# A literal order of pieces re-arranged in nine places, and idle products put in front of six waits of TensorE

## The chip, the cores and the metric

The kernel runs on one core of a Trainium2 chip. A core has TensorE (PE in the profile; its weight loads are PEld), VectorE (DVE), ScalarE (ACT), GpSimd (POOL) and SyncE (SP), and 16 DMA engines that all DMA queues share. The metric is device time in microseconds (us); lower is better. The kernel before was run four times: 711.54, 711.60, 713.12 and 713.61 us, median 712.36 us.

## The reference

Two feed-forward layers stand one behind the other, each behind a small conditioning step chosen by a number per batch. There are 8 batches of 512 tokens with 256 features.

```python
x = x + ffn0(cond0(x, lang0))     # low-rank products + embedding; int8-like rounding by one max over ALL of x and ALL of h
x = x + ffn1(cond1(x, lang1))     # adapter + layer norm; 9 experts, each token goes to its best 2
def ffn1(x):
    topk_w, topk_idx = top_k(softmax(x @ Wr), 2);  topk_w /= topk_w.sum()
    gate = silu(einsum('th,ehi->tei', xf, Wg));  hidden = gate * einsum('th,ehi->tei', xf, Wu)
    return einsum('tei,eih,te->th', hidden, Wd, cw)
```

Two facts set the shape of the work. The first layer's rounding of `h` needs one maximum over all batches, so nothing behind it can begin before the whole first half is done. And the second layer needs only 2 of 9 experts a token, so the kernel sorts tokens into lists by expert in DRAM and works on blocks of 128 list rows.

## The kernel before

**The front** (list `FRONT`, 8 batches in 4 pairs) makes the low-rank step, finds the maximum, rounds, and computes gate and up products (`gp`, `up`) into four PSUM tiles `wide` used in turn. `sl` and `uc` (ACT), `st` (DVE, L519) and `pm` (POOL) make `h`, and `mx` (DVE, L316) its maxima. At its end DVE joins the maxima (`htop_own`, L539), PE transposes that column (`across`, L320), a stretch of `ZEROS_BEHIND` idle products follows (`z`, L335: products of a tile of zeros into the `wide` tile that is next in turn), and DVE makes `htop` (L544) and the scale that every rounding of `h` needs.

**The literal order** (list `ORDER`) is a string of names written out by hand; each name runs one small function, and each engine gets its instructions in the order of the string. No planner changes it; semaphores follow from what each instruction reads and writes. The names, with batch b or block i behind them:

- `qa` (ACT, L624) and `qd` (DVE, L628) round `h`; `dp` (PE, L640) is the down product, `dv` (DVE, L647) adds it to x.
- `ap aa xp xa zp` make the adapter and the tokens' transposes (`xp` L693, `zp` L718), `zv` (DVE, L732) the norm's statistics, `np` (POOL, L739) and `nv` (DVE, L746) its scale, `na` (ACT, L756) and `nw` (DVE, L768) the normed rows, `tp` (PE, L776) and `ta` (ACT) their transposes.
- `cp ce ct cv` make the logits and the best two experts (`cv`, DVE, writes `both`, L830); `hp` (PE, L848 to L855) counts places from `both` and from `sofar`, `hv` (DVE, L861 to L874) makes the slots and the new `sofar`; `ca` writes the rows' tags.
- `hg` (POOL, L880) scatters 128 rows twice, by an indirect DMA each, into the DRAM tensor `lists`. There are 32 names, 64 DMAs.
- `pp`, `pw` plan which expert each block of 128 rows belongs to (`pp0b` is L959).
- For a block i: `R` (SP, L1052 to L1060) loads the block's place from SBUF into a register and issues five DMAs from `lists`; `U` and `W` (SP, L1067 and L1077) issue the expert's weights, 1408 KB and 768 KB, skipped when they are in place; `t` (DVE, L1088) transposes the rows; `g` in parts a, b, c (PE, L1098) is gate and up; `va vb vc vd` make `hidden`; `d` (PE, L1146) is the down product, `y` (DVE, L1152) weighs it, and `s` (POOL, L1156) adds the 128 rows to the output by an indirect DMA.

Blocks 0 to 13 are in the string; the others follow in a plain loop with the same pieces. Resources that bind names to each other:

```python
banks_sb = [psum.tile([P, 512], F32, name=f"bank{k}") for k in range(6)]   # dp ap tp cp ct hp pp g d, in turn
y_sb = [where_h_was(1, D) for _ in range(3)]                                # block i uses y_sb[i % 3]
...
nc.vector.tensor_scalar(y_sb[i % 3], held.pop(("po", i))[:, :D], ...)       # y, L1152
nc.gpsimd.indirect_dma_start(out=out, ..., in_=y_sb[i % 3], compute_op=ALU.add)   # s, L1156
own, `hg`:  out=own_rows[...]          # 64 disjoint views of `lists`
`R`:        lists[ds(r, P), quarter]   # a place known only at run time: any row of `lists`
```

So `y5` may write only when the transfer of `s2` has read the same tile, `y6` only behind `s3`. An `R` must wait for every `hg` that stands ahead of it in the string to have landed, and an `hg` for every `R` ahead of it to have read. One `s` waits for the landing of the one before it, since both add to `out`. SP has eight DMAs in the air at most, POOL also eight.

Of the kernel before, what the change touches and what calls it, by code (L numbers as in the profile page):

```python
# [32 lines left out]
P = 128  # L33
# [17 lines left out]
    up_2_3 mx_2_1 sl_2_3 up_2_4 mx_1_3 uc_2_3 up_3_0 st_2_4 gp_2_5 uc_3_0 pm_2_3 gp_3_0 mx_2_4 sl_2_5 up_2_5 up_3_1  # L51
    sl_3_0 st_2_5 gp_3_2 mx_2_5 uc_3_1 pm_3_0 mx_2_2 gp_3_1 sl_3_2 up_3_2 mx_2_3 sl_3_1 up_3_4 st_3_2 gp_3_5 pm_3_1
    uc_3_4 up_3_3 mx_3_0 sl_3_5 gp_3_4 mx_3_2 gp_3_3 sl_3_4 mx_3_1 up_3_5 sl_3_3 pm_3_4 st_3_5 st_3_3 mx_3_3 mx_3_4
    mx_3_5
"""
LAST_LOAD = "L_dT"
ZEROS_BEHIND = 12
ORDER = """
    qa0d fa1 fa0 fa2 qa0b qd0d qa0a qd0b qa0c fg0 fg1 qd0a qa2b qd0c dp0b qa1b qa1a dp0a qd1b dv0b qd1a dv0a dp1b
    qd2b qa2a xp0_1 dv1b xp0_0 ap0 xa0_1 qd2a xa0_0 dp1a qa2c xs0 aa0 qd2c qa4a zp0_0 dv1a zp0_1 zv0_0 qa3b ap1 fa3  # L60
    zv0_1 qa3a dp2a qd3b np0 aa1 qd3a dp2b dv2a pu1 pd0 nv0 dp3a dv2b na0_1 qd4a pu2 na0_0 nw0_1 xp1_1 ap2 qa4c
    xa1_1 nw0_0 xp1_0 qa4b zp1_1 dv3a xa1_0 tp0_0 pu0 aa2 zv1_1 zp1_0 ta0_0 qd4b tp0_1 qa5b zv1_0 dp3b ta0_1 qd4c
    np1 qa6b cp0 dv3b xs1 dp4b qd5b ce0 qa5a nv1 fa4 ct0 ap3 dv4b na1_1 mz0 cv0 dp4a na1_0 qa6c pd2 xp2_0 aa3 pd1
    xp2_1 nw1_1 hp0 ca0 fg2 xa2_1 hv0 tp1_1 xa2_0 zp2_1 ta1_1 xs2 nw1_0 hg0_0 zp2_0 zv2_1 tp1_0 fa5 ta1_0 zv2_0
    hg0_2 cp1 qd5a ce1 dv4a ct1 fg3 cv1 dp5b hg0_1 ap4 qd6b ca1 hp1 dv5b np2 aa4 dp5a hv1 qa6a hg0_3 nv2 pp0a qa7a
    pw0a dv5a pp0b pw0b na2_1 ap5 hg1_1 qd6a na2_0 pp0c qd6c nw2_1 dp6b qa7b hg1_3 nw2_0 xp3_1 xp3_0 xa3_1 pw0c fg4
    tp2_0 xa3_0 zp3_1 ta2_0 hg1_2 dv6b xs3 tp2_1 zv3_1 zp3_0 ta2_1 U0 qd7b cp2 aa5 zv3_0 hg1_0 ce2 fa6 dp6a qd7a
    ct2 dp7a dv6a np3 cv2 U1 dp7b W1 ap6 nv3 ca2 R0 dv7b na3_1 hp2 dv7a na3_0 xp4_0 hv2 xa4_0 xp4_1 nw3_0 R1 zp4_0
    xa4_1 zp4_1 nw3_1 tp3_0 aa6 t0 tp3_1 ta3_0 zv4_1 g0a W0 ta3_1 xs4 w0 zv4_0 fa7 cp3 va0 t1 hg2_1 g0b ce3 w1 fg5
    ct3 g0c vb0 np4 cv3 U2 g1a vc0 hg2_0 W2 nv4 g1b ca3 U3 vd0 va1 na4_1 hg2_2 g1c vb1 na4_0 nw4_1 d0 vc1 U4 hg2_3  # L70
    nw4_0 vd1 tp4_1 y0 xp5_0 ta4_1 s0 xp5_1 xa5_0 tp4_0 xa5_1 fg6 zp5_0 ta4_0 zp5_1 zv5_0 W3 cp4 zv5_1 ap7 ce4 R2
    ct4 np5 hp3 aa7 cv4 xs5 hv3 ca4 R3 nv5 hp4 hv4 na5_0 na5_1 t2 xp6_1 R4 w2 g2a xa6_1 nw5_0 nw5_1 tp5_0 va2 zp6_1
    ta5_0 t3 R5 d1 w3 zv6_1 t4 w4 tp5_1 y1 R6 xp6_0 ta5_1 s1 g2b xa6_0 zp6_0 vb2 W4 cp5 zv6_0 R7 g2c ce5 np6 g3a t5
    vc2 w5 nv6 vd2 ct5 xs6 na6_0 g3b U5 cv5 na6_1 d2 va3 fg7 hg3_3 nw6_1 ca5 nw6_0 hp5 W5 hg3_1 tp6_1 g3c hv5 ta6_1
    y2 tp6_0 vc3 U6 t6 xp7_0 hg4_0 ta6_0 w6 xp7_1 vb3 xa7_0 xa7_1 vd3 zp7_0 pp1a hg5_3 zv7_0 cp6 g4a ce6 pw1a xs7
    hg4_1 pp1b va4 g4b pw1b pp1c vb4 hg3_0 g4c pw1c d3 t7 vc4 U7 w7 hg3_2 vd4 g5a y3 W6 s2 d4 va5 hg4_3 g5b y4 W7
    s3 g5c vb5 hg4_2 g6a vc5 U8 vd5 hg5_2 g6b va6 g6c vb6 hg5_0 d5 vc6 U9 vd6 hg5_1 zp7_1 y5 ct6 W8 g7a zv7_1 s4
    cv6 d6 np7 va7 R8 nv7 ca6 na7_0 g7b s5 y6 na7_1 nw7_0 R9 hp6 g7c hv6 tp7_0 nw7_1 vc7 s6 ta7_0 R10 t8 tp7_1 w8
    g8a vb7 ta7_1 vd7 t9 d7 va8 w9 U10 R11 g8b y7 t10 s7 w10 cp7 vb8 g8c ce7 R12 ct7 g9a vc8 cv7 g9b va9 W10 t11
    ca7 U11 vd8 g9c w11 vb9 hg6_2 W9 d8 t12 vc9 w12 vd9 U12 hg6_1 g10a y8 W11 g10b s8 va10 hg6_3 g10c vb10 d9 vc10  # L80
    U13 vd10 hg6_0 g11a y9 W12 s9 d10 va11 R13 g11b y10 s10 g11c vb11 R14 g12a vc11 vd11 t13 d11 va12 w13 U14 R15
    g12b t14 y11 s11 g12c vb12 W14 hp7 vc12 R16 g13a hv7 vd12 pp2a va13 g13b pw2a R17 pp2b vb13 d12 pw2b W13 pp2c
    y12 U15 g13c pw2c s12 W15 vc13 hg7_3 U16 vd13 hg7_0 hg7_1 hg7_2
"""
BLOCKS_IN_ORDER = 14

# [2 lines left out]
def adaln_ffn_kernel(  # L89
# [21 lines left out]
    nc = tc.nc  # L111

    B, _, KC, S = xT.shape
# [21 lines left out]
    def act_scale(top, sig, name):  # L135
# [27 lines left out]
    start = rt.tile([P, NJ, E], F32, name="start")  # L163
    nc.gpsimd.iota(
        start, pattern=[[0, NJ], [CAP, E]], base=0, channel_multiplier=0, allow_small_or_imprecise_dtypes=True
# [13 lines left out]
    wdT = l0.tile([P, NM, D], BF16, name="wdT")  # L179
# [26 lines left out]
    turn_of = {}  # L206
# [35 lines left out]
    with tc.tile_pool(name="hw", bufs=1) as hw, tc.tile_pool(  # L242
# [75 lines left out]
        def across(pi, col, n, i):  # L318

            nc.tensor.transpose(pi[:, i : i + n], col.to_broadcast([n, P]), ident[:n, :n])  # L320
# [9 lines left out]
        @front  # L330
        def z(n):

            pz = wide_sb[(turn_of.get("wide", -1) + 1) % len(wide_sb)]
            for _ in range(n):
                nc.tensor.matmul(pz[:, :S], lhsT=busy[:, :P], rhs=busy, start=True, stop=True)  # L335
# [205 lines left out]
        across(ph, own, P, 0)  # L541
        z(ZEROS_BEHIND)
        htop = l0.tile([P, 1], F32, name="htop")
# [8 lines left out]
    banks_sb = [psum.tile([P, 512], F32, name=f"bank{k}") for k in range(6)]  # L552
# [615 lines left out]


    @piece  # L1170
    def pu(i, k):
        rows_of = slice(LIKELY[i] * P, (LIKELY[i] + 1) * P)
        nc.sync.dma_start(gu_sb[i].rearrange("p c n -> p (c n)"), Wx[rows_of, : KC * GU])
# [147 lines left out]
```

## Time and profile before

| what | value |
|---|---|
| median of four runs | 712.36 us |
| the profiled execution | 713.14 us, of which 711.4 us from its first to its last instruction |
| mean granted TensorE clock | 0.971 |
| PE busy | 667.4 us, 94% |
| first half (`FRONT`) ends, across-transpose of `htop_own` | 83.74 us |
| first expert product `g0a` | 157.17 us |
| `g2a` | 184.25 us |
| `g8a` | 253.23 us |
| largest waits of PE | 7.6, 5.3 and 4.7 us |

How to read it: a view of waits lists, for an engine, who ended its idle time; a timeline has start, duration, engine, line, operation and the idle time before it; a view of stretches gives the busy time of each engine between two times and the granted clock (1.00 is full). From 253 to 703 us PE works through the blocks without a wait that the waits' view names.

### The profile page before, as it was taken

The numbers are of one execution on the slowest core, as the hardware profiler recorded it, in microseconds if no ns is written. First come the engines' busy times: TensorE is split into PE (matmuls) and PEld (weight loads), VectorE is DVE, ScalarE is ACT, GpSimd is POOL, SyncE is SP. The second block draws the span as 40 slices with busy tenths as digits, with TensorE's granted clock in tenths as the row PEclk, the third lists the DMA queues.
The fourth block names the chain that finished last, engine by engine and source line by source line (L and its number), as shares of the span: only waits on it lengthen the run. The fifth ranks groups of instructions, "written<-read, shape, count | busy, mean of one in ns | idle before, by whom it ended". The sixth has DMA issues, their size and how long they took to land. (4 is left out here: it accounts for less than half of the span.)

```text
span 711.4 us, 14642 instructions
## 1 busy us (share of the span) xinstructions
PE 667.4 (94%) x4688; PEld 564.9 (79%) x4688; DVE 337.7 (47%) x1036; ACT 201.7 (28%) x407; POOL 206.8 (29%) x190
## 2 busy tenths in 40 slices
PE   9989798869799689999999999999999999999995
PEld 3333245448689589999999999999999999999994
DVE  3989868866673352433333333333333233333331
ACT  4697687634341121111111111111111111111110
POOL 1036313716164726161121121211211212212112
PEclk9999899889899979999999999999999999999998
DMA  8600039557379765233475332399624696225832
GB/s 337 218 15 1 0 100 381 192 185 231 78 252 389 238 149 160 45 84 54 110 224 129 90 54 47 85 311 310 197 42 113 162 289 202 46 51 141 244 81 33
DMA packets 86641, 107.91 MB, mean 152 GB/s; under 512 B 58904, under 2 KB 75424, under 8 KB 82976
## 3 DMA queue, kind: packets, MB, share of 16 engines
q1 hardware_dynamic: 73696, 89.61, 39.5%
q0 software_dynamic: 12720, 17.31, 12.5%
q8 instruction: 39, 0.64, 0.3%
q14 instruction: 42, 0.34, 0.1%
q10 hardware_dynamic: 144, 0.01, 0.0%
HBM read 183.55 MB, written 22.83 MB: 290 GB/s over the span
## 5 line engine op out<-in xcount | busy, mean ns | idle before, releaser
L1098 PEld LDWEIGHTS bank<-upper__104,lower 128*128 128x128 f32 x2636 | 310.2, 194 | 9.1 <-DVE upper__104 L1088 5.0
L1098 PE MATMUL bank<-upper__104,lower 128*128 128x128 f32 x2636 | 313.0, 278 | 4.7 <-DVE upper__104 L1088 4.7
L1156 POOL DMA_INDIRECT out_dram<-upper__104,tag x67 | 103.9, 1550 | 364.6 <-DVE upper__104 L1088 263.5
L1114 DVE TENSOR_TENSOR upper__104<-bank,upper__104 128x512 f32<-128x512 f32 x67 | 46.3, 691 | 163.1 <-PE bank L1098 159.4
L1108 ACT ACTIVATE upper__104<-bank 128x512 f32<-128x512 f32 x67 | 40.0, 597 | 236.4 <-PE bank L1098 228.8
L880 POOL DMA_INDIRECT lists<-row,sloti x64 | 63.8, 997 | 48.4 <-issue 17.1
L1146 PE MATMUL bank<-upper__104 128*128 128x256 f32 x312 | 71.6, 379 | 0.0
L1146 PEld LDWEIGHTS bank<-upper__104 128*128 128x128 f32 x312 | 57.4, 190 | 6.8
L1146 PE MATMUL tok<-upper__104 128*128 128x256 f32 x216 | 49.6, 379 | 0.0
L1146 PEld LDWEIGHTS tok<-upper__104 128*128 128x128 f32 x216 | 39.7, 190 | 4.6
L1124 ACT ACTIVATE upper__104<-bank 128x128 f32<-128x128 f32 x41 | 11.4, 277 | 107.3 <-PE bank L1098 107.3
L1146 PE MATMUL bank<-lower,upper__104 128*128 128x256 f32 x180 | 41.5, 380 | 0.1
L1152 DVE TENSOR_SCALAR upper__104<-bank,wt 128x256 f32<-128x256 f32 x41 | 19.8, 484 | 45.5 <-PE bank L1146 45.5
L1098 PE MATMUL tok<-upper__104,lower 128*128 128x128 f32 x312 | 39.1, 275 | 0.0
L1098 PEld LDWEIGHTS tok<-upper__104,lower 128*128 128x128 f32 x312 | 36.9, 192 | 0.0
L1146 PEld LDWEIGHTS bank<-lower,upper__104 128*128 128x128 f32 x180 | 33.0, 190 | 4.3 <-issue 0.4
L1130 DVE TENSOR_TENSOR upper__104<-bank,upper__104 128x128 f32<-128x128 f32 x41 | 11.8, 289 | 39.5 <-ACT upper__104 L1125 38.3
L1124 ACT ACTIVATE upper__104<-tok 128x128 f32<-128x128 f32 x26 | 7.2, 278 | 65.5 <-PE tok L1098 65.5
L506 ACT ACTIVATE g<-wide,swg 128x1024 f32<-128x1024 f32 (+1 forms) x24 | 24.1, 1038 | 3.1 <-PE wide L482 2.8
L1152 DVE TENSOR_SCALAR upper__104<-tok,wt 128x256 f32<-128x256 f32 x26 | 12.6, 484 | 21.4 <-PE tok L1146 21.4
L640 PE MATMUL bank<-yq,wdT 128*128 128x512 bf16 x80 | 21.5, 402 | 1.2 <-ACT ha L678 0.5
L1130 DVE TENSOR_TENSOR upper__104<-tok,upper__104 128x128 f32<-128x128 f32 x26 | 7.6, 291 | 31.7 <-ACT upper__104 L1125 31.7
(215 smaller groups left out, 705.8 us busy)
## 6 DMA issues: line engine op xcount, KB each, us to landing
lower<-in_L_ffn_W_dram SPq DMA_DIRECT2D x73, 1408.0 KB
upper__104<-in_L_ffn_W_dram SPq DMA_DIRECT2D x48, 768.0 KB
lower<-in_L_ffn_W_dram SPq DMA_DIRECT2D x24, 768.0 KB
lower<-lists SPq DMA_DIRECT2D x144, 32.0 KB
upper__104<-lists SPq DMA_DIRECT2D x140, 32.0 KB
x_sb<-in_x_dram SPq DMA_DIRECT2D x8, 512.0 KB
out_dram<-xtok SPq DMA_DIRECT2D x8, 512.0 KB
lists<-pad SPq DMA_DIRECT2D x10, 130.0 KB
```

The costliest lines, as they stand in the source:

```text
L506: nc.scalar.activation(g, pg, AF.Silu, scale=swg[:, m : m + 1])
L640: nc.tensor.matmul(pd, lhsT=wdT[:, m, cs], rhs=hq_sb[b % 2][:, m], start=m == 0, stop=False)
L880: nc.gpsimd.indirect_dma_start(out=own_rows[(b * NJ + j) * 2 + n], out_offset=bass.IndirectOffsetOnAxis(ap=sloti_sb[b % 3][:, j, n : n + 1 ...
L1098: nc.tensor.matmul(pg[:, at * P : (at + 1) * P], lhsT=gu_sb[i % NW][:, c, n * P : (n + 1) * P], rhs=xbT_sb[i % 3][:, c], start=c == 0, sto ...
L1108: nc.scalar.activation(g_sb[i % 3][:, :4].rearrange("p m t -> p (m t)"), held.pop(("pg", i, "a")), AF.Silu)
L1114: nc.vector.tensor_tensor(hid_sb[i % 3][:, :4].rearrange("p m t -> p (m t)"), held.pop(("pg", i, "b")), g_sb[i % 3][:, :4].rearrange("p m ...
L1124: nc.scalar.activation(gs[:, 4], pg[:, :P], AF.Silu)
L1130: nc.vector.tensor_tensor(hid[:, 4], pg[:, P : 2 * P], gs[:, 4], ALU.mult)
L1146: nc.tensor.matmul(po[:, :D], lhsT=hid_sb[i % 3][:, m], rhs=dn_sb[i % NW][:, m], start=m == 0, stop=m == NM - 1)
L1152: nc.vector.tensor_scalar(y_sb[i % 3], held.pop(("po", i))[:, :D], small_["wt"][i % NX], None, ALU.mult)
L1156: nc.gpsimd.indirect_dma_start(out=out, out_offset=bass.IndirectOffsetOnAxis(ap=tag_sb[i % NX][:, 0:1].bitcast(I32), axis=0), in_=y_sb[i % 3],
```

## The change

In `FRONT` a last name `z_22` is added: 22 idle products behind the last real one. `ZEROS_BEHIND` goes from 12 to 24. A new piece `zz` issues n products of a weight tile with itself (128x128 by 128x512, bf16) into the bank that is next in turn, without taking it; nothing reads them.

```diff
-    mx_3_5
+    mx_3_5 z_22
-ZEROS_BEHIND = 12
+ZEROS_BEHIND = 24
+    @piece
+    def zz(n, k):
+
+        pz = banks_sb[(turn_of.get("bank", -1) + 1) % len(banks_sb)]
+        for _ in range(n):
+            nc.tensor.matmul(pz, lhsT=wdT[:, 0, :P], rhs=wdT[:, :2].rearrange("p m d -> p (m d)"), start=True, stop=True)
```

In `ORDER` five names `zz` are added and nine names move. The strings, cut to where they differ (the diff itself is re-wrapped lines):

```diff
- dv5a pp0b pw0b
+ dv5a zz5 pp0b pw0b
- np3 cv2 U1 dp7b W1 ap6 nv3 ca2 R0 dv7b
+ np3 cv2 R0 U1 dp7b W1 ap6 nv3 ca2 dv7b
- R3 nv5 hp4 hv4 na5_0 na5_1 t2 xp6_1 R4
+ R3 nv5 zz8 hp4 hv4 na5_0 na5_1 t2 zz4 xp6_1 R4
- g5a y3 W6 s2 d4 va5 hg4_3 g5b y4 W7 s3 g5c vb5 hg4_2 g6a vc5 U8 vd5 hg5_2 g6b va6 g6c vb6 hg5_0 d5 vc6 U9 vd6 hg5_1 zp7_1 y5 ct6 W8 g7a zv7_1 s4 cv6 d6 np7 va7 R8 nv7
+ g5a y3 W6 hg4_3 hg4_2 hg5_2 hg5_0 hg5_1 d4 va5 g5b y4 W7 g5c vb5 g6a vc5 U8 vd5 g6b va6 g6c vb6 d5 vc6 U9 vd6 zp7_1 s2 y5 ct6 W8 g7a zv7_1 np7 s3 s4 cv6 d6 va7 R8 nv7
- g7c hv6 tp7_0 nw7_1 vc7 s6 ta7_0 R10 t8 tp7_1 w8 g8a
+ g7c hv6 zz3 tp7_0 nw7_1 vc7 s6 ta7_0 R10 t8 zz6 tp7_1 w8 g8a
```

So `R0` goes ahead of `U1` and `W1` on SP. On POOL five `hg` (ten scatters) go ahead of `s2` and `s3`, `s2` to just ahead of `y5`, and `np7` ahead of `s3` and `s4`. Idle products added: 22 + 12 + 5 + 8 + 4 + 3 + 6 = 60.

More of the change, by code (lines that the diff above doesn't have):

```diff
@@ L53 @@
     uc_3_4 up_3_3 mx_3_0 sl_3_5 gp_3_4 mx_3_2 gp_3_3 sl_3_4 mx_3_1 up_3_5 sl_3_3 pm_3_4 st_3_5 st_3_3 mx_3_3 mx_3_4
-    mx_3_5
+    mx_3_5 z_22
 """
 LAST_LOAD = "L_dT"
-ZEROS_BEHIND = 12
+ZEROS_BEHIND = 24
 ORDER = """
[L59 to L83, printed above, removed]
@@ new lines @@
+    qa0d fa1 fa0 fa2 qa0b qd0d qa0a qd0b qa0c fg0 fg1 qd0a qa2b qd0c dp0b qa1b qa1a dp0a qd1b dv0b qd1a dv0a dp1b qd2b
+    qa2a xp0_1 dv1b xp0_0 ap0 xa0_1 qd2a xa0_0 dp1a qa2c xs0 aa0 qd2c qa4a zp0_0 dv1a zp0_1 zv0_0 qa3b ap1 fa3 zv0_1
+    qa3a dp2a qd3b np0 aa1 qd3a dp2b dv2a pu1 pd0 nv0 dp3a dv2b na0_1 qd4a pu2 na0_0 nw0_1 xp1_1 ap2 qa4c xa1_1 nw0_0
+    xp1_0 qa4b zp1_1 dv3a xa1_0 tp0_0 pu0 aa2 zv1_1 zp1_0 ta0_0 qd4b tp0_1 qa5b zv1_0 dp3b ta0_1 qd4c np1 qa6b cp0 dv3b
+    xs1 dp4b qd5b ce0 qa5a nv1 fa4 ct0 ap3 dv4b na1_1 mz0 cv0 dp4a na1_0 qa6c pd2 xp2_0 aa3 pd1 xp2_1 nw1_1 hp0 ca0 fg2
@@ new lines @@
+    xa2_1 hv0 tp1_1 xa2_0 zp2_1 ta1_1 xs2 nw1_0 hg0_0 zp2_0 zv2_1 tp1_0 fa5 ta1_0 zv2_0 hg0_2 cp1 qd5a ce1 dv4a ct1 fg3
+    cv1 dp5b hg0_1 ap4 qd6b ca1 hp1 dv5b np2 aa4 dp5a hv1 qa6a hg0_3 nv2 pp0a qa7a pw0a dv5a zz5 pp0b pw0b na2_1 ap5
+    hg1_1 qd6a na2_0 pp0c qd6c nw2_1 dp6b qa7b hg1_3 nw2_0 xp3_1 xp3_0 xa3_1 pw0c fg4 tp2_0 xa3_0 zp3_1 ta2_0 hg1_2
+    dv6b xs3 tp2_1 zv3_1 zp3_0 ta2_1 U0 qd7b cp2 aa5 zv3_0 hg1_0 ce2 fa6 dp6a qd7a ct2 dp7a dv6a np3 cv2 R0 U1 dp7b W1
+    ap6 nv3 ca2 dv7b na3_1 hp2 dv7a na3_0 xp4_0 hv2 xa4_0 xp4_1 nw3_0 R1 zp4_0 xa4_1 zp4_1 nw3_1 tp3_0 aa6 t0 tp3_1
@@ new lines @@
+    ta3_0 zv4_1 g0a W0 ta3_1 xs4 w0 zv4_0 fa7 cp3 va0 t1 hg2_1 g0b ce3 w1 fg5 ct3 g0c vb0 np4 cv3 U2 g1a vc0 hg2_0 W2
+    nv4 g1b ca3 U3 vd0 va1 na4_1 hg2_2 g1c vb1 na4_0 nw4_1 d0 vc1 U4 hg2_3 nw4_0 vd1 tp4_1 y0 xp5_0 ta4_1 s0 xp5_1
+    xa5_0 tp4_0 xa5_1 fg6 zp5_0 ta4_0 zp5_1 zv5_0 W3 cp4 zv5_1 ap7 ce4 R2 ct4 np5 hp3 aa7 cv4 xs5 hv3 ca4 R3 nv5 zz8
+    hp4 hv4 na5_0 na5_1 t2 zz4 xp6_1 R4 w2 g2a xa6_1 nw5_0 nw5_1 tp5_0 va2 zp6_1 ta5_0 t3 R5 d1 w3 zv6_1 t4 w4 tp5_1 y1
+    R6 xp6_0 ta5_1 s1 g2b xa6_0 zp6_0 vb2 W4 cp5 zv6_0 R7 g2c ce5 np6 g3a t5 vc2 w5 nv6 vd2 ct5 xs6 na6_0 g3b U5 cv5
@@ new lines @@
+    na6_1 d2 va3 fg7 hg3_3 nw6_1 ca5 nw6_0 hp5 W5 hg3_1 tp6_1 g3c hv5 ta6_1 y2 tp6_0 vc3 U6 t6 xp7_0 hg4_0 ta6_0 w6
+    xp7_1 vb3 xa7_0 xa7_1 vd3 zp7_0 pp1a hg5_3 zv7_0 cp6 g4a ce6 pw1a xs7 hg4_1 pp1b va4 g4b pw1b pp1c vb4 hg3_0 g4c
+    pw1c d3 t7 vc4 U7 w7 hg3_2 vd4 g5a y3 W6 hg4_3 hg4_2 hg5_2 hg5_0 hg5_1 d4 va5 g5b y4 W7 g5c vb5 g6a vc5 U8 vd5 g6b
+    va6 g6c vb6 d5 vc6 U9 vd6 zp7_1 s2 y5 ct6 W8 g7a zv7_1 np7 s3 s4 cv6 d6 va7 R8 nv7 ca6 na7_0 g7b s5 y6 na7_1 nw7_0
+    R9 hp6 g7c hv6 zz3 tp7_0 nw7_1 vc7 s6 ta7_0 R10 t8 zz6 tp7_1 w8 g8a vb7 ta7_1 vd7 t9 d7 va8 w9 U10 R11 g8b y7 t10
@@ L84 @@
+    s7 w10 cp7 vb8 g8c ce7 R12 ct7 g9a vc8 cv7 g9b va9 W10 t11 ca7 U11 vd8 g9c w11 vb9 hg6_2 W9 d8 t12 vc9 w12 vd9 U12
+    hg6_1 g10a y8 W11 g10b s8 va10 hg6_3 g10c vb10 d9 vc10 U13 vd10 hg6_0 g11a y9 W12 s9 d10 va11 R13 g11b y10 s10 g11c
+    vb11 R14 g12a vc11 vd11 t13 d11 va12 w13 U14 R15 g12b t14 y11 s11 g12c vb12 W14 hp7 vc12 R16 g13a hv7 vd12 pp2a
+    va13 g13b pw2a R17 pp2b vb13 d12 pw2b W13 pp2c y12 U15 g13c pw2c s12 W15 vc13 hg7_3 U16 vd13 hg7_0 hg7_1 hg7_2
 """
```

## The prediction

> **What bounds the kernel now.** I read the page first, then PE's waits, then the timelines of PE, SP, POOL and DVE around each wait. (a) The page: PE is busy 94%, and the clock's thin slices (9 is full) all lie in the first 14 of 40, up to 249 us.
>
> ```profile
> PE 667.4 (94%) x4688; PEld 564.9 (79%) x4688; DVE 337.7 (47%) x1036; ACT 201.7 (28%) x407; POOL 206.8 (29%) x190
> ...
> PEclk9999899889899979999999999999999999999998
> ```
>
> (b) PE's waits: the three long ones are, in this order, the places of `tp7_0`, of `z_22` and of `g0a` behind `t0`; `hp4` follows with 2.2 us.
>
> ```profile
> PE bank L776 <- DVE place L861: 7.6, 1, 7.6
> PE wide L320 <- DVE htop_own L539: 5.3, 1, 5.3
> PE bank L1098 <- DVE upper__104 L1088: 4.7, 1, 4.7
> ```
>
> From 253 us on PE has no wait, so the end moves by what `g8a`'s start (253.23) moves, plus what the clock does behind it. The question is therefore not how many waits are filled but what decides `g8a`. (c) Two stretches, 84 to 89 and 250 to 256 us, have the granted clock at 0.50 (third number from the end of each line), each behind a wait.
>
> ```profile
> 84.00:89.00 5.00, 5.00 (x13) 1.81 (x12) 1.94 (x7) 3.91 (x5) 0.00 (x0) 0.50 0.00 0
> 250.00:256.00 6.00, 4.61 (x21) 4.24 (x22) 4.70 (x18) 1.17 (x2) 1.59 (x1) 0.50 0.60 86
> ```
>
> **Part 1, `z_22` and 24 zeros: +1.5 us.** Timeline rows of the front:
>
> ```profile
> 78.56 1.94 DVE L519 SCALAR_TENSOR_TENSOR upper__104<-wide,swu,g 128x512 f32<-128x512 f32 x2
> ...
> 83.74 0.47 PE L320 MATMUL wide<-ident,htop_own 128*128 128x128 f32 x1 [5.32 <-DVE htop_own L539]
> 84.01 5.33 PE L335 MATMUL wide<-busy 128*128 128x512 bf16 x12
> ```
>
> One idle product at full clock costs 0.215 us (x12 take 2.75 us, x4 1.03 us: 1.72/8). `z_22` writes the `wide` tile next in turn. Counting the turns in `FRONT`, that is `up_3_3`'s, which `st_3_3` reads until 78.56+1.94 = 80.50. So the fillers cannot start at 78.4, when PE falls idle, but at 80.55; 22 of them and the step to a transpose (the existing `z_10` at 27.82, its transpose at 30.11: 2.29 for ten, so 0.14 beside 10 x 0.215) put the transpose at 85.42 instead of 83.74. It runs at full clock, 0.32 instead of 0.47, so `htop` is 1.53 late, and the roundings with it. The 24 zeros start 0.16 later and end at 85.58 + 24 x 0.215 = 90.74; `dp0b` started at 89.39 behind twelve at half clock. So 1.35 on PE, 1.53 on ACT and DVE: I take 1.5. No gain stands against it, as `dp0b` already ran at full clock. Fourteen fillers would have been free ((83.74 - 80.55 - 0.14)/0.215). All of the kernel behind waits for `htop`, so this shift passes on; the times of parts 2 and 3 are on the clock of before, without it.
>
> **Part 2, `R0` ahead of `U1`, `W1`: early gain, no lasting one.**
>
> ```profile
> 147.56 0.38 SPq L1077 DMA_DIRECT2D upper__104<-in_L_ffn_W_dram  x1
> 149.03 1.92 SPq L1057 DMA_DIRECT2D lower<-lists  x4
> ...
> 156.80 0.51 DVE L1088 STREAM_TRANSPOSE upper__104<-lower 128x128 f32<-128x128 f32 x2 [5.07 <-DMA lower<-lists]
> ```
>
> U1 and W1 (1408 and 768 KB) stand ahead of R0 on SP's queue, and its rows land at 156.7. Moved, R0 issues from 146.3 (register load from 144.9; `hg1` had landed by 145.0 in the semaphore record) and lands by 149.6, so `t0` follows `nw3_1` at 151.75 and `g0a` starts at 152.2 instead of 157.17. But R0 takes 3.6 us of SP (147.94 to 151.52), so U1 and W1 go from 146.84 to 150.4, finish at 159.5 instead of 155.9, and R1, queued behind them, lands its rows at 160.3 instead of 158.3. `g1a` waits for `t1`: 160.8, still 4.0 earlier than 164.8. The `hg2` scatters wait until R1 has read: 161.5 instead of 159.70. R2 waits for `hg2` to land: about 179.2 instead of 178.03. `g2a` then starts near 182.9 instead of 184.25, and if `zz8`, `zz4` hold the clock (0.50 from 184 to 188 before) it gains 2 more. SP issues R2 to R7 back to back (178.03 to 198.75) and `hg3_3` waits until R7 has read, 201.21: it goes to 202.4, **1.2 later**. From 184 to 242 PE so runs 1.4 to 3.4 ahead, but what POOL does is 1.2 behind.
>
> `zz5` (1.1 us in a 0.7 us wait) delays `pp0b` 0.4, hidden because DVE reads its result only after `dv5a` (ends 132.59): 0. `zz8`, 1.7 us, fits in 2.2; `zz4`, 0.9 us, in 1.3: 0.
>
> **Part 3, the POOL order, where `g8a` is decided.**
>
> ```profile
> 217.81 0.96 POOL L880 DMA_INDIRECT lists<-row,sloti  x1 [0.30 <-issue]
> ...
> 244.45 0.86 POOL L739 TENSOR_SCALAR va<-mv 128x4 f32<-128x4 f32 x1
> ```
>
> Before, `np7` (244.45) stands behind s2 (222.61), s3 (231.11), the ten scatters between and behind them, and s4 (243.43); nv7, na7, nw7 and the transposes follow: `tp7_0` 249.87, `g8a` 253.23. Now the ten `hg` scatters run on from 217.81 at 1.265 us each: the last ends at 231.4, plus 1.2, 232.6, and `s2` issues at 232.9 where it did at 222.6. Then the new wait: `y5` shares a tile with `y2`, so DVE holds `y5` until s2 has landed, and `zv7_1`, `cv6`, `nv7`, `y6`, `nw7` all stand behind `y5` on DVE. Before, `y5` waited on s2's semaphore as well, but that had landed at 230.36, ahead of `d5`. How long does a scatter take to land? The DMA view, by stretch (220 to 243 us, then 243 to 256; median us from issue to landing at the end):
>
> ```profile
> out_dram<-upper__104,tag POOLq DMA_INDIRECT x2, 7.7
> ...
> out_dram<-upper__104,tag POOLq DMA_INDIRECT x3, 3.9
> ```
>
> 7.7 with weights on the queues, 3.9 without. W8 runs to 242.5 before and, asked for 2 us earlier but beside ten more scatters, to about 241 now; I take 7.7 for s2, 3.9 for s3. So: s2 lands 240.65; `y5` to 241.2; `zv7_1` (1.15) to 242.35; `np7` (1.45 from there, as in 177.56 to 179.0) to 243.8; `s3` issues 244.1 and lands 248.0; `y6`, same tile as `y3`, 248.05 to 248.55; `nw7_0` to 249.9 (before: 249.72); `hv6`, `nw7_1`, `t8` 2.4+0.4 behind as before; `g8a` 253.4. Change: **+0.2**. The stall has moved from np7 to the two landings, and the 1.4 to 3.4 us that PE has in hand are waited away there. `zz3` lies in that wait: 0. `zz6` takes 1.3 us in a 1.39 wait at full clock, but 2.6 at half, +0.8 then; against that, products right before `g8a` may bring the clock back for its 3.5 us, -1.6. I leave these two out of the sum and in the range (-1.6 to +0.8).
>
> **A rule weighed.** The scatter row says 7.7 us beside weight loads. The Trainium skill, "DMA: Bandwidth & Descriptors" (Anatomy of one DMA, SWDGE path), gives about 2.0 us plus bytes/436 GB/s; for 128 KB that is an estimate of 2.3 us, and the same page (Queues, rings and completion order) lets an engine take turns between queues. By it s2 would land at 235.2, `g8a` come 5 us sooner, and the change be faster. The row is from this very stretch, so I go by it.
>
> **A second rule.** The gate closed behind 119.95 to 123.36 us with PE busy 2.22 us, and not behind 130.20 to 133.60 with 2.26. "TensorE: Matmul & The Clock Gate" (PE-mode transpose) says transposes do not count as activity, which fits, as the first stretch holds more of them. It speaks against counting busy time, and for plain products as fillers.
>
> **Sum.** 1.5 + 0.2 = +1.7 us. The profiled execution took 713.14 (711.4 and 1.74 around), so it becomes 714.8. It lies 0.8 above the median; on the median, 712.36 + 1.7 = 714.1 us, +0.24%. This measurement can tell about 0.3% (2.1 us) from no change.
>
> **Rivals.**
> 1. *Forecast, no change (0.42)*: 714.1; with landing times of s2 from 239.5 to 241.5 and the clock's two terms 712 to 716.
> 2. *Slower: the clock falls in front of the transpose (0.22).* PE is idle 2.15 us (78.4 to 80.55). The half-clock stretches last 6.83 or 10.24 us, multiples of 3.41, so the gate seems to count in windows of that length. If one ends so that this idle time fills enough of it, `z_22` runs at half clock; and up to one window, 3.4 us, is lost ahead of `htop`: 714.1 + 3.4 = 717.5. It decides from about two thirds of a window idle. For it: an empty window closed the gate here before. Against: 38.03 to 41.44, busy 1.82 of 3.41 us, did not.
> 3. *Slower: the scatters land later than 7.7 (0.18).* Twenty-four in a row at 1.265 us, each needing the landing of the eighth before it (10.1 us): two more us on s2 give 716.1 and more. It decides from 8.4 us on.
> 4. *Faster: the queues are empty when s2 goes (0.18).* Landing after 3.9: -3.8, so 710.3, and 708.7 with `g8a` at full clock. For it: W8 is asked for earlier. Against: 24 scatters stand ahead of it.
> That all early gains reach the end (4 to 8 us) would need `y5` not to wait for s2; the tile's turn of three excludes it.
>
> Faster by over 0.3%: 0.18; within: 0.42; slower: 0.40. The range 709.0 to 717.5 takes in rivals 3 and 4 and the edge of 2; the likeliest case alone is 712 to 716.
>
> **What would show it.** Right: the transpose of `htop_own` near 85.4; `g0a` about 3.5 us earlier (-5.0+1.5), `hg3_3` near 204; `y5` near 242, long after `d5`; `tp7_0` waiting about as long as now in sum. Wrong: `g8a` far below 250 us (s2 landed fast), or a transpose before 84 (the fillers did not wait for the tile).

## The result and the profile after

| | before | after |
|---|---|---|
| median | 712.04 us (78 runs, 707.55 to 716.58) | 713.93 us (52 runs, 710.57 to 718.24) |
| ratio to before | 1 | 1.003, 95% interval 1.0019 to 1.004 |
| the profiled execution, its span | 713.14, 711.4 us | 711.22, 709.4 us |
| mean granted clock of it | 0.971 | 0.988 |

The changed kernel takes 0.3% longer, about 2 us. Executions of one and the same kernel lie 8 to 9 us apart, and the profiled execution of after is a short one, 2.7 us under its median. So the two profiles show which wait stands where, and the medians what it costs; the difference of the two profiled times (-1.9) shows neither. The ratios, and the counts over profiles further down, leave out executions more than 1.5% above the shortest of their kernel, and a ratio, being estimated by itself, can lie up to 0.2% beside the quotient of the two medians.

Line numbers of after are one lower than those of before (g is L1097, y L1151, s L1155, zz L1174). The page of after, the rows that answer to those of before:

```profile
PE 671.6 (95%) x4748; PEld 566.2 (80%) x4748; DVE 337.5 (48%) x1036; ACT 201.6 (28%) x407; POOL 207.2 (29%) x190
...
PEclk9999999999999799999999999999999999999999
```

PE is busier, as it has 60 idle products more, and of the six slices that were under 9 in the row of the clock one is left, the one of `y5`'s wait. PE's waits:

```profile
PE bank L847 <- DVE both L829: 9.8, 2, 9.3
PE bank L1097 <- DVE upper__104 L1087: 2.6, 2, 2.1
...
PE wide L334 <- DVE upper__104 L518: 2.1, 1, 2.1
```

The wait of 7.6 us in front of `tp7_0` has become one of 9.3 us in front of `hp6`, which stands a few pieces ahead of it in the order and needs `both` of `cv6`, a DVE piece behind `y5`. The 5.3 us in front of the transpose are 2.1 us and 22 fillers. The timeline of PE in the front (start, duration, the idle time before in brackets):

```profile
79.67 4.91 PE L334 MATMUL wide<-busy 128*128 128x512 bf16 x22 [2.13 <-DVE upper__104 L518]
84.42 0.27 PE L319 MATMUL wide<-ident,htop_own 128*128 128x128 f32 x1
84.52 5.34 PE L334 MATMUL wide<-busy 128*128 128x512 bf16 x24
89.92 1.24 PE L639 MATMUL bank<-yq,wdT 128*128 128x512 bf16 x5
```

The fillers wait for `st_3_3` (L518), as the forecast had it. This execution came to the end of its last real product 0.89 us sooner than before's (77.53 against 78.42), so distances from there are what can be compared: transpose 6.88 us behind it against 5.32, `dp0b` 12.39 against 10.97. At this point after runs 0.53 us late (89.92 against 89.39).

The timelines of POOL, DVE and PE where `g8a` is decided, one row of each that matters:

```profile
230.78 1.61 POOL L1155 DMA_INDIRECT out_dram<-upper__104,tag  x1 [0.30 <-issue]
...
244.08 1.64 POOL L1155 DMA_INDIRECT out_dram<-upper__104,tag  x1 [0.20 <-issue]
```

```profile
240.86 0.48 DVE L1151 TENSOR_SCALAR upper__104<-bank,wt 128x256 f32<-128x256 f32 x1 [13.78 <-DMA out_dram<-upper__104,tag]
...
247.82 0.48 DVE L1151 TENSOR_SCALAR upper__104<-bank,wt 128x256 f32<-128x256 f32 x1 [2.31 <-DMA out_dram<-upper__104,tag]
```

```profile
252.26 0.63 PE L775 MATMUL bank<-ident,row 128*128 128x128 f32 x4 [0.56 <-DVE row L767]
252.72 1.95 PE L1097 MATMUL bank<-upper__104,lower 128*128 128x128 f32 x16
```

In the kernel before, `y5` on DVE waited for `d5`, and `g8a` on PE ran at half clock:

```profile
233.42 0.48 DVE L1152 TENSOR_SCALAR upper__104<-bank,wt 128x256 f32<-128x256 f32 x1 [1.31 <-PE bank L1146]
```

```profile
253.23 3.50 PE L1098 MATMUL bank<-upper__104,lower 128*128 128x128 f32 x16
```

Now `s2` starts at 230.78, and DVE stands idle for 13.78 us in front of `y5`, until 240.86, when `s2` has landed. `y6` waits for `s3` (244.08 to 247.82). `g8a` comes 0.51 us earlier than before (1.04 without the 0.53) and runs at full clock, 1.95 us instead of 3.50. The stretches of the prediction's second view, now at clock 1.00 (third number from the end):

```profile
84.00:89.00 5.00, 5.00 (x25) 2.38 (x24) 1.94 (x7) 3.44 (x5) 0.00 (x0) 1.00 0.00 0
250.00:256.00 6.00, 5.44 (x37) 4.33 (x36) 4.62 (x17) 1.77 (x3) 0.64 (x1) 1.00 0.83 258
```

### The profile page after: what moved, and what is told of

The parts are those of the page before. It is cut to its first block, busy times and chain, and to the rows that moved or that the text cites. A ratio compares the mean times of both kernels' runs of the same rounds, so it can differ in the third digit from the quotient of the medians.

```text
span 709.4 us, 14761 instructions
## 1 busy us (share of the span) xinstructions
PE 671.6 (95%) x4748; PEld 566.2 (80%) x4748; DVE 337.5 (48%) x1036; ACT 201.6 (28%) x407; POOL 207.2 (29%) x190
## 5 line engine op out<-in xcount | busy, mean ns | idle before, releaser
L1097 PEld LDWEIGHTS bank<-upper__104,lower 128*128 128x128 f32 x2636 | 308.1, 193 | 7.1 <-DVE upper__104 L1087 3.0
L1097 PE MATMUL bank<-upper__104,lower 128*128 128x128 f32 x2636 | 311.2, 277 | 2.6 <-DVE upper__104 L1087 2.6
L1155 POOL DMA_INDIRECT out_dram<-upper__104,tag x67 | 104.3, 1557 | 356.4 <-DVE upper__104 L1087 274.7
L1151 DVE TENSOR_SCALAR upper__104<-bank,wt 128x256 f32<-128x256 f32 x41 | 19.8, 483 | 55.8 <-PE bank L1145 39.7
L1097 PE MATMUL tok<-upper__104,lower 128*128 128x128 f32 x312 | 39.1, 275 | 0.0
L1097 PEld LDWEIGHTS tok<-upper__104,lower 128*128 128x128 f32 x312 | 36.9, 192 | 0.0
L334 PE MATMUL wide<-busy 128*128 128x512 bf16 x90 | 22.8, 407 | 3.8 <-DVE upper__104 L518 2.1
L1151 DVE TENSOR_SCALAR upper__104<-tok,wt 128x256 f32<-128x256 f32 x26 | 12.6, 483 | 21.4 <-PE tok L1145 21.4
```

What stands on the lines that cost most here:

```text
L1097: nc.tensor.matmul(pg[:, at * P : (at + 1) * P], lhsT=gu_sb[i % NW][:, c, n * P : (n + 1) * P], rhs=xbT_sb[i % 3][:, c], start=c == 0, sto ...
L1155: nc.gpsimd.indirect_dma_start(out=out, out_offset=bass.IndirectOffsetOnAxis(ap=tag_sb[i % NX][:, 0:1].bitcast(I32), axis=0), in_=y_sb[i % 3],
```

## The experiments

The theory: the change moves a stall. What holds `g8a` is the landing of `s2` and `s3`, because `y5` and `y6` write the tiles that these read; and the fillers of the front delay the transpose. Its rivals: the clock that the fillers keep up pays for them, or the wait is not of the tile but of something as late behind it. Each kernel ran beside the kernel before on the same chip; a ratio below is to that. Where positions are compared, they are the starts of `y` on DVE against those of before's profile; `y1` to `y4` lie 0.2 to 1.1 us later there in 2, 4 and 9, whose literal order is unchanged up to them, so a microsecond says nothing.

**1. After without its part in the front.**

```diff
-    mx_3_5 z_22
+    mx_3_5
-ZEROS_BEHIND = 24
+ZEROS_BEHIND = 12
```

> The changed kernel without its part in the front: no z_22, twelve zeros as before; all else as changed. Theory (the fillers wait for the tile that st_3_3 reads, and put the transpose 1.5 us late): transpose of htop_own 5.9 us behind the start of the last front product instead of 7.5, time 1.5 us below the changed kernel, so about 712.4 us, ratio to before 1.0005. Rival A (the fillers pay by the clock: without them the half-clock stretch at 82 to 89 us comes back and costs more than they do): as the changed kernel or slower, 714 us or more. Rival B (the cost of the change sits in the stretch from 220 to 255 us alone): as the changed kernel, 713.9.

712.03 us, ratio 1.0003 (0.9972 to 1.0034). As the theory had it, 1.9 us under after's median. The interval reaches up to the rivals' 713.9 and 714, so the time alone does not exclude them; the trace shows the mechanism, and experiment 2 the price.

```profile
81.62 0.47 PE L319 MATMUL wide<-ident,htop_own 128*128 128x128 f32 x1 [5.32 <-DVE htop_own L538]
81.89 4.14 PE L334 MATMUL wide<-busy 128*128 128x512 bf16 x12
```

The transpose is again 5.32 us behind the last real product. The half-clock stretch came back (81.3 to 84.7), and cost little: the twelve zeros took 4.14 us, `dp0b` began 9.85 us behind that product.

**2. Before with the front's part alone.**

> The kernel before with the front's part alone: z_22 and 24 zeros. Theory: transpose 7.5 us behind the start of the last front product, half-clock stretch at 82 to 89 us gone, time +1.5 us, about 713.5, ratio 1.002. Rival A (the clock pays): 712.0 or less, ratio 1.000 or below. Rival B (the 34 products of the front cost their whole 7.3 us): 719, ratio 1.010.

717.14 us against 712.37, ratio 1.0052 (1.0029 to 1.0076): slower than the theory's 1.002, far from Rival B. Its timeline of PE shows why:

```profile
78.57 6.59 PE L335 MATMUL wide<-busy 128*128 128x512 bf16 x21 [2.13 <-DVE upper__104 L519]
85.00 0.27 PE L320 MATMUL wide<-ident,htop_own 128*128 128x128 f32 x1
```

The fillers take 6.59 us here and 4.91 in after: the clock was at half from 79.9 to 83.3, from 1.3 us behind their start, after 2.1 us in which PE had waited. That is Rival 2 of the prediction. The transpose stands 8.56 us behind the last real product. Over the profiled executions of this study (without that of 7, which has 6.88 and 12.39 too), the kernels with `z_22` have 6.88 three times and 8.56 or 8.57 twice, `dp0b` 12.39 and 14.07 or 14.08; the seven without have 5.32 each time, `dp0b` 10.97 or 10.98 four times and 9.85 to 10.10 three times. The means of `dp0b` are 13.06 and 10.56: by these profiles the part in the front costs 2.5 us, not 1.5. Five and seven executions are few; the three ratios (after, 1, 2) give 1.9 to 3.7.

**3. After with six y tiles.**

```diff
-    y_sb = [where_h_was(1, D) for _ in range(3)]
+    y_sb = [where_h_was(1, D) for _ in range(6)]
-        nc.vector.tensor_scalar(y_sb[i % 3], ...     # and in s
+        nc.vector.tensor_scalar(y_sb[i % 6], ...
```

> The changed kernel with six y tiles instead of three (block i uses tile i mod 6), all else as changed. Theory (what holds g8a is that y5 and y6 wait until the scatters s2 and s3 have landed): y5 follows d5 at about 232, DVE's wait of 13.8 us goes, np7 follows zv7_1 at about 234, and g8a waits next for the rows of R8, whose last load is issued at 239 and takes some 3 to 4 us to land: g8a at 243 to 245 instead of 252.7, time 7 to 9 us below the changed kernel, 705 to 707, ratio to before 0.990 to 0.993. Rival A (the wait moves on: rows or weights of block 8, or POOL's queue, are as late): g8a at 250 or later, 712 to 714. Rival B (PE is bound behind 253 us by loads, so that what is won at g8a is waited for again at a later block): g8a early, and the time still above 710, with a new wait of PE behind 260 us.

711.48 us, ratio 0.9979 (0.9948 to 1.001). The wait is what the theory says, and the time is Rival B's. DVE's and PE's timelines:

```profile
229.11 0.48 DVE L1151 TENSOR_SCALAR upper__104<-bank,wt 128x256 f32<-128x256 f32 x1 [1.31 <-PE bank L1145]
```

```profile
242.34 2.05 PE L1097 MATMUL bank<-upper__104,lower 128*128 128x128 f32 x16 [1.61 <-DVE upper__104 L1087]
```

`y5` follows `d5`, `g8a` starts 10.4 us earlier than in after. But behind `g8a`, up to 400 us, PE now has waits that neither kernel has:

```profile
PE bank L952 <- DVE sofar L873: 3.8, 1, 3.8
PE bank L1097 <- DMA lower<-in_L_ffn_W_dram: 2.2, 1, 2.2
PE bank L1145 <- DMA lower<-in_L_ffn_W_dram: 1.8, 1, 1.8
```

Against before, `y6` is 12.7 us early, `y9` 10.1, `y11` 3.3, `y12` 4.8, `y20` 4.8, `y24` 0.8, and it stays there. Two more bounds stand behind the first one: the last plan (`pp2a`, L952), which needs `hv7`, on DVE behind the transposes of the rows that R13 and R14 load, and R13 waits for the scatters `hg6`; and weights at 367 us that SP asks for at 361, behind a write of padding rows.

**4. Before with six y tiles.** The same edit on the kernel before.

> The kernel before with six y tiles, nothing else. Theory: before the change y5 did not wait for a landing (s2 had landed ahead of d5), and np7 stood behind the scatters on POOL, so nothing moves: 712.0, ratio 1.000, within 0.2%. Rival (the three tiles already held the kernel before): 2 us or more faster, ratio 0.997 or below.

712.92 us, ratio 0.9998 (0.9974 to 1.0021), and PE's first wait is as before (`PE bank L776 <- DVE place L861`, 8.6 us). The three tiles bind only once the order has put `s2` late.

**5 to 8, a chip on which the kernel before takes longer.** Four kernels ran on a chip where the kernel before takes 728.92 us (723.76 to 737.65), 2.3% more.

5 is before with `R0` alone moved:

> The kernel before with R0 alone moved ahead of U1 and W1. Theory (g8a is set by POOL's chain from hg3_3 over the scatters to np7, and that chain is held by R7's reading, not by g0a): g0a 5 us earlier, every block up to 4 some 4 to 5 us earlier, hg3_3 0 to 1.2 us later, g8a at 253 to 254.5 with a wait of PE in front of it that is 4 us longer; time 712 to 713.5, ratio 1.000 to 1.002. Rival (an early gain of PE reaches the end): 707 to 709, ratio 0.993 to 0.996.

6 is before with POOL's names alone moved:

> The kernel before with POOL's names alone moved (five hg ahead, s2 to just ahead of y5, np7 ahead of s3 and s4); no idle products, R0 as before. Theory with the landing that the changed kernel showed (10.1 us from s2's start to y5, 3.7 from s3 to y6): last hg ends near 231.4, s2 starts 231.7, y5 at 241.8, np7 243.5, s3 245.1, y6 248.9, g8a 253.8 against 253.2: +0.6, time 712.6, ratio 1.001. With the 7.7 us of the prediction: g8a 251.5, -1.7, ratio 0.9976. Rival (the three names in front of np7 were the whole of the wait, and y5's wait is hidden): g8a near 246, ratio 0.990.

7 is experiment 3 with this edit in the loop behind the string:

```diff
         ask(i + 1 + AHEAD, 0, 0)
-        if behind_rows:
-            behind_rows()
         ask(0, i + 1 + NW, i + NW - 1)
+        if behind_rows:
+            behind_rows()
```

> The changed kernel with six y tiles, and in the loop of the blocks from 14 on the nine writes of padding rows (lists<-pad, on SP) stand behind the weights of the same block instead of ahead of them. Theory (of the 12.7 us won at y6 by six tiles, 4 were lost at block 21, whose weights are issued only at 361 because SP waits for a padding write's turn): the load is asked 2 to 3 us earlier, PE's wait of 2.2 us for it and the half-clock stretch behind it go, gain of 4.8 us at block 13 lasts to the end: 707 to 708, ratio 0.993 to 0.995. Rival A (SP's chain as a whole, or the DMA engines at 98% in that stretch, sets when these weights land): as the kernel with six tiles, 711 to 712, the wait for weights still there. Rival B (the padding writes now hold up the next rows): a new wait of PE for t or g between 330 and 450 us, 711 or more.

8 is experiment 3 with the scatters `hg6` ahead of `s7` and `s8`:

```diff
- y7 t10 s7 w10 ... hg6_2 ... hg6_1 ... y8 W11 g10b s8 va10 hg6_3 ... hg6_0 g11a
+ y7 t10 w10 ... hg6_2 ... hg6_1 ... y8 W11 g10b va10 hg6_3 ... hg6_0 s7 s8 g11a
```

> The changed kernel with six y tiles, and on POOL the eight scatters hg6 ahead of s7 and s8. Theory (of the 12.7 us won at y6 by six tiles, 8 were lost before block 12, because R13 waits for hg6, and hg6 stands behind s7, which waits for the landing of s6): hg6 starts at 258 to 260 instead of 265.4, R13 at 272 to 274 instead of 278.9, PE's wait of 3.8 us at the last plan goes, y12 is 8 to 11 us earlier than before the change instead of 4.8; if block 21's weights come earlier by as much, because the last scatters and so SP's chain of padding writes start earlier, the time is 704 to 708, ratio 0.988 to 0.994. Rival (block 21's weights land at 367 whatever happens here): y12 early and the time still 711 to 712, with a longer wait for weights at 360 to 370.

Measured: 729.18 (ratio 0.9997, 0.9961 to 1.0033), 739.34 (1.0131, 1.008 to 1.0183), 734.91 (1.008, 1.0039 to 1.0121) and 735.99 us (1.0102, 1.0062 to 1.0142). What differs there can be seen inside a run of equal products, here PE in the kernel of 6:

```profile
175.92 0.38 PE L1145 MATMUL bank<-lower,upper__104 128*128 128x256 f32 x1 [0.21 <-issue]
176.63 0.47 PE L1145 MATMUL bank<-lower,upper__104 128*128 128x256 f32 x1 [0.34 <-issue]
177.34 0.38 PE L1145 MATMUL bank<-lower,upper__104 128*128 128x256 f32 x1 [0.24 <-issue]
```

PE waits between single products for nothing that the profile shows, and DVE stands idle once for 13.7 and once for 9.3 us with a releaser that the profile calls only remote. `y5` in 6 waited for `d5`, not for `s2`. So these four say little on the theory: `R0` alone is no gain there, and what lost 0.8 to 1.3% in the other three is open. The kernels of 5, 6 and 8 were run again; the edit of 7 was run again only together with others, in 10.

**9. POOL's names alone, on a chip of the usual time** (kernel before there: 712.47).

```diff
- y3 W6 s2 d4 va5 hg4_3 ... s3 ... hg4_2 ... hg5_2 ... hg5_0 ... hg5_1 zp7_1 y5 ... s4 cv6 d6 np7
+ y3 W6 hg4_3 hg4_2 hg5_2 hg5_0 hg5_1 d4 va5 ... zp7_1 s2 y5 ... np7 s3 s4 cv6 d6
```

> The kernel before with POOL's names alone moved (five hg ahead, s2 to just ahead of y5, np7 ahead of s3 and s4), as once before, now beside its own runs of the kernel before. Theory, with the landing that the changed kernel showed (10.1 us from s2's start to y5, 3.7 from s3 to y6): y5 at 241.8, np7 243.5, s3 245.1, y6 248.9, g8a about 253.8 against 253.2: +0.6, ratio 1.001. With the 7.7 us of the prediction: g8a 251.5, -1.7, ratio 0.9976. If the chip's transfers are slow, so that the kernel before takes 725 or more: s2 lands over 12 us behind its start and the ratio is 1.005 or more.

712.84 us, ratio 1.0011 (0.9991 to 1.0032): the theory's number. POOL, then DVE:

```profile
232.68 1.61 POOL L1155 DMA_INDIRECT out_dram<-upper__104,tag  x1 [0.30 <-DVE upper__104 L1129]
```

```profile
242.82 0.48 DVE L1151 TENSOR_SCALAR upper__104<-bank,wt 128x256 f32<-128x256 f32 x1 [9.92 <-DMA out_dram<-upper__104,tag]
```

10.14 us from `s2` to `y5`, as in after (10.08). The profiled execution is a long one, 716.08 us, and its `g8a` stands at 255.39, 1.6 us later than expected, so positions are better counted from the start of `hg3_3`, ahead of which nothing differs from before. From there to `g8a` are 53.2 us here, 52.5 in after and 54.4 in 1; with POOL's old order 52.0 in before, and 53.7, 53.7 and 54.2 in 4, 11 and 2. Moving POOL's names takes `np7` out of one queue and puts `y5` behind one landing; the two weigh the same.

**10. After with four things: six y tiles, `hg6` first, the padding writes behind, `z_14` for `z_22`.**

> The changed kernel with four things: six y tiles, the scatters hg6 ahead of s7 and s8, the padding writes behind the weights of their block, and in the front z_14 instead of z_22. Theory (the early gain was lost one after the other at y5 and y6, at R13 behind hg6, and at the weights of block 21): transpose of htop_own 5.9 us behind the start of the last front product, at full clock, g8a 9 to 11 us earlier than before the change, hg6 at 258 to 260, y12 8 to 12 us earlier, no wait for weights at 360 to 370, time 701 to 705, ratio 0.985 to 0.990. Rival A (the weights of block 21 land near 367 whatever is moved): 709 to 711, ratio 0.996 to 0.998, wait for weights of 2 us or more there. Rival B (fourteen fillers too delay the transpose): transpose 6.3 us or more behind that start.

704.18 us, ratio 0.9906 (0.9879 to 0.9933), faster than both kernels. In the profile `y6` is 14.1 us early, `y9` 10.8, and 10.8 it stays to the end; no wait for weights is left. POOL:

```profile
255.59 1.55 POOL L1155 DMA_INDIRECT out_dram<-upper__104,tag  x1 [6.62 <-issue]
258.31 1.00 POOL L879 DMA_INDIRECT lists<-row,sloti  x1 [1.16 <-DVE wt L1139]
```

`hg6` starts at 258.31 and not behind `s7`, which would wait for `s6` to land. And the front:

```profile
79.61 3.18 PE L334 MATMUL wide<-busy 128*128 128x512 bf16 x14 [2.13 <-DVE upper__104 L518]
82.80 0.32 PE L319 MATMUL wide<-ident,htop_own 128*128 128x128 f32 x1
```

82.80 is 5.32 behind the last real product, at full clock: fourteen fillers cost the transpose nothing, as the prediction worked out. This is one execution; what fourteen cost when the clock falls in them is not shown.

**11. Before with `R0` alone, on a chip of the usual time** (kernel before there: 712.74).

```diff
- np3 cv2 U1 dp7b W1 ap6 nv3 ca2 R0 dv7b
+ np3 cv2 R0 U1 dp7b W1 ap6 nv3 ca2 dv7b
```

> The kernel before with R0 alone moved ahead of U1 and W1, as once before, now on a chip of the usual time if the kernel before takes about 712. Theory (POOL's chain to np7 sets g8a, and hg3_3, which heads it, waits for R7's reading): g0a 5 us earlier, blocks 0 to 5 earlier by 4 to 5 us, hg3_3 between 1 us earlier and 1.2 later, g8a within 1 us of 253.2; time 711.5 to 713.5, ratio 0.999 to 1.002. Rival (the early gain of PE reaches the end): ratio 0.993 to 0.996.

713.64 us, ratio 1.0011 (0.9989 to 1.0034). `g0a` starts at 153.20 instead of 157.17, and PE's longest wait grows from 7.6 us to

```profile
PE bank L775 <- DVE place L860: 11.1, 1, 11.1
```

The 4 us won at `g0a` are waited away in front of `tp7_0`, 90 us later. Two expectations missed: `y1` to `y4` are 2.0 us earlier than before, not 4 to 5, and `g8a` stands at 254.66, 1.4 us later and not within 1.

**12. After with six y tiles and `hg6` first**, the kernel of 8.

> The changed kernel with six y tiles and the scatters hg6 ahead of s7 and s8; front and padding writes as in the changed kernel. Theory (hg6 held R13, and the padding writes hold the weights of block 21): y12 some 9 us earlier than before the change as in the kernel with all four, but the weights of block 21 are asked some 5 us later than there, PE waits 2 to 5 us for them, and the time lies between: 706 to 709, ratio 0.992 to 0.996. Rival A (hg6 alone was enough, its earlier end brings SP's chain forward): no wait at block 21, 704 to 706 (the front's 1.5 us more than the kernel with all four), ratio 0.989 to 0.991. Rival B (without the padding writes moved nothing is won): 711, ratio 0.998.

705.17 us, ratio 0.9892 (0.9862 to 0.9922): Rival A. The order of the padding writes and the fourteen fillers add nothing that the intervals of 10 and 12 could tell apart; what the padding writes alone are worth stays open. In the profiled execution, the longest of six (707.9), the clock fell in the fillers again (8.56), `y6` is 9.8 us early, PE waits 2.5 us for weights in front of `d9`, and 5.3 us are left to the end, where some 9 were expected at `y12`.

## Why the prediction was right, point by point

The forecast was 714.1 us, +0.24%; measured were 713.93 and +0.3%, which 52 runs tell from no change. The case that came is the likeliest one. Its sum held partly by luck, because errors cancelled: the front cost more than its term, and in part 3 one term was too late by what the other was too short.

- **Part 1, +1.5: right for one state of the clock, too small on the whole.** Transpose +1.56 (forecast 1.68), `dp0b` +1.42 (1.35) in after's profile. Left out of the sum: with `z_22` the clock fell inside the fillers in two executions of five, 1.7 us more, which was Rival 2 at a chance of 0.22 and a price of 3.4; and without it the twelve zeros ran partly at full clock in three executions of seven, so that `dp0b` came 0.9 to 1.1 sooner than in the profile that the sum was made on. On the mean that makes 2.5 us. The Trainium skill, "TensorE: Matmul & The Clock Gate" (What's actually happening), calls the window free-running and the count of slow products different from run to run; the two outcomes of one and the same front agree with that.
- **Part 2, no lasting gain: right, with a wrong term in it.** Counted from the start of `nw3_0` on DVE (148.99 in before, 149.90 in 11), `g0a` follows after 3.3 us in six profiles with `R0` moved, and after 8.1 to 8.5 in four without: 4.8 to 5.2 earlier, forecast 5.0. The start of `hg2` is 1.8 later in 11 (forecast 1.8). But R2, forecast 1.2 later, is not later: from the last `hg2` to R2 are 5.4 us instead of 7.9. In both traces R2 issues within a microsecond of the end of a stretch of full DMA engines (about 177.6 in before, 178.1 in 11); that the weights moving there hold the scatters back is argued, not shown. So **`hg3_3` was not 1.2 us late**: from `nw3_0` to it are 51.1 to 52.9 us with `R0` moved and 51.1 to 52.3 without. The sign named for it, a start near 204, did not come (200.25).
- **Part 3, y5 behind the landing of s2: the mechanism right, its term too small.** From `s2` to `y5` are 10.1 us in after and in 9, where the sum took 7.7; from `s3` to `y6` 3.7 in after and 4.0 in 9, where it took 3.9. The start of `s2`, 232.9 in the sum, is 230.25 without the front's 0.53, and all of that difference stands already at `hg3_3` (202.4 in the sum, 199.7): from there to `s2` are 30.5 us in both. So 2.65 us too late and 2.35 us too short: `y5` came at 240.3, counted the same way, forecast 240.65. The landing is past the 8.4 us from which Rival 3 was to decide; its loss did not come because `s2` started earlier than the sum had it. That the two errors are of one size is luck.
- **The rule weighed there.** The Trainium skill, "DMA: Bandwidth & Descriptors" (Anatomy of one DMA, SWDGE path), gave an estimate of 2.3 us for such a scatter. The trace has 10.1 and 3.7; the measurement decides, and the row of the same stretch, though too low, was the nearer one.
- **`zz6`: the range's better end in after, but no rule.** `g8a` at full clock gains 1.55 us in after. With `zz6` it took 1.95, 1.95 and 2.05 us in after, 1 and 3, but 3.18 and 3.52 in 10 and 12, where PE waited another 1.7 to 1.8 us right before it (1.6 in 3); without `zz6` 2.92 to 3.62 in before, 2, 4, 9 and 11. No run has the fillers alone, so what they gain is not shown. In after they delayed nothing: behind `zz5`, `zz8`, `zz4`, `zz3` and `zz6` PE still waited 0.28 to 0.56 us for other engines. In 1 `zz6` itself ran at half clock, 2.77 us, and PE did not wait behind it.
- **What the rivals' last sentence said.** That the early gains would reach the end if `y5` did not wait for `s2` was half true: `y5` no longer waits in 3, and of 12.7 us at `y6` only 0.8 are left by `y24`. It took `hg6` ahead of `s7` as well (12, 10).

Still open: how the spread of 8 us between executions of one kernel is made up; the clock's stretches differ between profiles of the same front, and so are likely a part of it. And the five `zz` were never run by themselves: from `dp0b` to `nw3_0` five profiles with `zz5` take 58.2 to 60.2 us and five without 59.6 to 62.4, so a gain that the sum put at nothing may hide there; after made up its 0.53 us and 0.8 more in that stretch.

## What to carry to other kernels

A stage that waits can have several bounds close behind each other, as this one had three: take the first away in an experiment and read the next from the waits before you count its gain. When an instruction is moved ahead in one engine's order, look for what its buffer makes wait: three y tiles cost nothing before the change and held `g8a` back by 10 us after it. Filler products are free only between the moment when their target tile is released and the moment when the real product is ready; count that stretch, not the whole idle time, and leave out what does not fit.

## What the runs showed of the hardware

- The same indirect scatter of 128 rows had landed 10.1 us after its start in after, with 24 other scatters issued right ahead of it, and 3.7 us after its start a few microseconds later. Two stretches of after (the last two numbers of a line are the DMA engines' share and GB/s):

```profile
230.00:243.00 13.00, 5.49 (x38) 4.99 (x37) 2.01 (x10) 0.60 (x1) 2.48 (x4) 0.84 0.83 300
243.00:249.00 6.00, 4.17 (x26) 3.26 (x26) 3.34 (x20) 2.98 (x10) 3.53 (x3) 0.50 0.33 49
```

  Whether the scatters ahead or the weights beside it made the first one long, no run separates.
- The same fillers, at the same distance from the same product and behind the same 2.1 us of idle time, took 4.91 us in three profiled executions and 6.59 or 6.60 in two, in which the clock was at half for 3.4 us.
- One chip took 2.3% longer for the kernel before; there PE idled 0.2 to 0.3 us between single products of one block, with no releaser in the profile. The ratio to the kernel before on the same chip carried over for `R0` alone (0.9997 and 1.0011), but not for two kernels whose order depends on landings: 1.0131 there and 1.0011 elsewhere for 6 and 9, 1.0102 and 0.9892 for 8 and 12.
